# A transformer block on one core: GpSimd's elementwise work on VectorE, a norm's squares in two slots, the fold of a maximum in its own slot, weights fetched one step ahead

## The chip, the core and the metric

The kernel runs on one core of a Trainium2 chip. Its engines have the names of the profile: PE multiplies matrices, DVE (VectorE) and ACT (ScalarE) work element by element, POOL is GpSimd, SP only issues transfers. The metric is the device time of one execution in microseconds; the time before is a median of three runs.

## The reference

The input `x` is float32, 4 sequences of 1024 rows of 512 (D). A vector of 128 numbers for each sequence gives scale `g` and shift `b` of two norms.

```python
def norm(x, t, gw, gb, bw, bb):
    g = (t @ gw.T + gb)[:, None, :]
    b = (t @ bw.T + bb)[:, None, :]
    return g * x * rsqrt(mean(x * x, axis=-1) + 1e-6) + b

def attention(x):                       # 16 heads of 32
    q, k, v = heads(x @ Wq.T), heads(x @ Wk.T), heads(x @ Wv.T)
    p = softmax(q @ k.T / sqrt(32))
    return merge(p @ v) @ Wo.T

def swiglu(x):                          # hidden size 2048
    return silu(x @ gate_w.T) * (x @ hid_w.T) @ out_w.T

x2 = x + attention(norm(x, t, g1w, g1b, b1w, b1b))
out = x + x2 + swiglu(norm(x2, t, g2w, g2b, b2w, b2b))
```

## The kernel before

All tensors lie with features on the 128 partitions, in C = 4 chunks, and with rows on the free axis. The 4096 rows form 8 blocks (`n`) of 512, two for each sequence (`b`, `half`).

**The main loop.** One step `g` handles the scores of four heads, 256 queries and two tiles of 128 keys: `scores(g)` on PE into the one scores bank of PSUM, `keep(g)` on ACT, which copies them to a tile `raw` (nine buffers), and `running_max(g)` on DVE. Four steps (`kind = g % 4`) make a unit `j`: four heads, 256 queries, all 1024 keys. A block has 32 steps and the loop 256, with ten more to drain it. What follows for a unit is spread over later steps:

- `fold_max(j)` halves the running maximum on DVE, `max_T` transposes it on PE (tile `mt`, in the scores bank), `parts` and `parts_T` split it into three bfloat16 parts and transpose them back, `spread` broadcasts the result to `shift`. All of it stands in the kind-0 and kind-1 steps of the next unit.
- Five steps after its scores, `shifted(r)` subtracts the maximum on DVE and `exponential(r)` follows on ACT. One step later `weighted(r)` multiplies by the values on PE and `accumulate(r)` adds the tile into the first `raw` tile of the unit by an accumulating DMA issued from POOL.
- `fold_sum`, `sums` (PE), and `normalize(j)` (a reciprocal on DVE and a multiply on POOL, which writes `oT`) finish the unit.

**What fills PE.** Between these pieces the loop places chains of matmuls into PSUM, 16 short ones each (`mm` splits a matmul into four of 32 columns). They come from two lists: `queue` (projections of keys, queries and values, then the feed-forward `hidden` and `contract` of finished blocks) and `first` (four output projections `project_out` of a block, due eight steps after the block's end). A credit gives two chains per step at the start and 1.6 later. One chain stands in the middle of a step and is evicted there; the other, `late`, stands at its end and is evicted at the start of the next step. Each chain's result occupies one of three PSUM buffers until its eviction: on ACT in the projections (`st`, `sv`), on DVE or on ACT and DVE in the feed-forward part (`h`, `res`).

**The norms.** `norm_squares` makes four squares on ACT and adds them on POOL, `norm_root` averages them with a matmul (`pm`) and takes the root on ACT, `norm_inverse` and `norm_scale` multiply by its reciprocal on DVE, `norm_mod` applies `g` and `b` on ACT. For the attention norm of later sequences (`y`) they hang at steps before `s`, for the feed-forward norm (`x2`) at steps `g0+10` to `g0+16`, where `g0` is the step at which the block's attention steps have ended. `after` hangs a piece at a step's end, `between` in its middle, `pin` at its start.

**Order and queues.** PE, DVE, ACT and POOL execute their instructions in the order in which the program records them. SP's queue (all weight and activation loads and stores) is ordered by the tile framework. Weights of `wkq`, `wo` and `fw` share three buffers. A weight load is recorded with the chain that uses it first.

Of the kernel before, what the change touches and what calls it, by code (L numbers as in the profile page):

```python
# [17 lines left out]
P = 128  # L18
# [6 lines left out]
def tile_cond_transformer_block(  # L25
# [82 lines left out]
    def norm_squares(dst, tag: str):  # L108
        total = None
        for c in range(C):  # L110
            sq = sb.tile([P, NB], F32, tag="t", name=f"sq{tag}_{c}", bufs=3)
            nc.scalar.activation(sq, dst[:, c, :], AF.Square)
            if c == 0:
                total = sb.tile([P, NB], F32, tag="tot", name=f"tot{tag}", bufs=1)
                first = sq
            elif c == 1:
                nc.gpsimd.tensor_tensor(total, first, sq, ALU.add)
            else:
                nc.gpsimd.tensor_tensor(total, total, sq, ALU.add)  # L119
        state[tag] = total  # L120
# [11 lines left out]
    def norm_scale(dst, tag: str):  # L132
        inv = state.pop(tag)
        for c in range(C):
            nc.vector.tensor_tensor(dst[:, c, :], dst[:, c, :], inv, ALU.mult)
# [22 lines left out]
    def norm_rest(which: int, b: int, dst, tag: str):  # L158
        inv = state.pop(tag)
        for c in range(C):  # L160
            nc.vector.tensor_tensor(dst[:, c, :], dst[:, c, :], inv, ALU.mult)
            norm_mod(which, b, dst, c)
# [180 lines left out]

    def normalize(j: int):

        m, qh = divmod(j, NB // HQ)
        n, hg = divmod(m, C)
        rec = sb.tile([P, HQ], F32, tag="rec", name=f"rec{j}", bufs=2)
        nc.vector.reciprocal(rec, state.pop(("sum", j)))  # L349
        if qh == 0:  # L350
            oT[n, hg] = sb.tile([P, NB], F32, tag=f"oT{hg}", name=f"oT{m}")
        nc.gpsimd.tensor_tensor(oT[n, hg][:, qh * HQ : (qh + 1) * HQ], avs.pop(j), rec, ALU.mult)  # L352
# [5 lines left out]
    def project_out(n: int, d: int):  # L358
# [10 lines left out]
        def evict():  # L369
            nc.vector.tensor_tensor(x2[n][:, d, :], pp, res[n][:, d, :], ALU.add)  # L370
            nc.gpsimd.tensor_tensor(res[n][:, d, :], res[n][:, d, :], x2[n][:, d, :], ALU.add)
# [11 lines left out]
    def hidden(n: int, f: int, a: int):  # L383

        if a == 0:
            load_f(n, f)
# [49 lines left out]
    def chains_of(b: int, half: int):  # L436
        todo = []
        for hg in range(C):
            todo.append((load_wkq, project_kq, (b, hg, 0, half)))
# [10 lines left out]
    for hg in range(1, C):  # L450
        enqueue(0, load_wkq, project_kq, (0, hg, 0, 0))
        enqueue(0, None, project_kq, (0, hg, 0, 1))
        enqueue(0, None, project_kq, (0, hg, 1, 0))
    for hg in range(C):
        enqueue(0, load_wkq, project_kq, (0, hg, 1, 1))
    for b in range(1, B):
        for half in range(QB):
# [4 lines left out]
            pin(s - 9, load_y, b, half)  # L462
            after(s - 7, lambda b=b, half=half, tag=tag: norm_squares(y[b, half], tag))
            between(s - 5, norm_root, tag)
            after(s - 4, norm_inverse, tag)
            after(s - 3, lambda b=b, half=half, tag=tag: norm_scale(y[b, half], tag))
            for c in range(C):
                after(s - 2 + c // 2, lambda b=b, half=half, c=c: norm_mod(0, b, y[b, half], c))
            for load, fn, a in chains_of(b, half):
                enqueue(s, load, fn, a)  # L470
    for n in range(NBLK):
# [4 lines left out]
        if n < NBLK - 1:  # L476
            tag = f"f{n}"
            after(g0 + 10, lambda n=n, tag=tag: norm_squares(x2[n], tag))
            between(g0 + 12, norm_root, tag)
            after(g0 + 13, norm_inverse, tag)  # L480
            after(g0 + 14, lambda n=n, tag=tag: norm_scale(x2[n], tag))
# [5 lines left out]
        for g in range(NF // FG):  # L487
            for k in range(FG):
                for a in range(2):
                    enqueue(g1, None, hidden, (n, g * FG + k, a))  # L490
# [4 lines left out]
    for m in range(NBLK * C):  # L495
        pin(m * MS + 4, load_v, m)

    def chain(g: int):
# [5 lines left out]
        if load is not None:  # L504
            load(a[1])
        return fn(*a)

    with tc.manual_schedule(
# [8 lines left out]
        load_modw(1)  # L517
        norm_sum(y[0, 0], "a0_0")
# [27 lines left out]
        while g < NR + 10 or pinned or ended:  # L546
# [13 lines left out]
            if kind == 0 and n_on:  # L560
                normalize(j_n)
            if kind == 3 and s_on:
                fold_sum(j_s)
            if x_on and kind != 1:
                shifted(r_x)
            if late is not None:
                late()
                late = None
            for fn, a in pinned.pop(g, []):
# [14 lines left out]
            if kind == 0 and m_on:  # L584
                fold_max(j_m)
# [10 lines left out]
            if evict is not None:  # L596
                evict()
            for fn, a in halfway.pop(g, []):
# [78 lines left out]
```

## Time and profile before

| | before |
|---|---|
| median of three runs | 2567.27 us (2566.82 to 2568.72) |
| profiled execution, its own time | 2566.51 us |
| span of its profile | 2564.7 us |
| busy: PE, DVE, ACT, POOL | 2470.7, 1764.4, 1309.0, 457.0 us |
| mean granted clock of PE | 0.991 |
| accumulating transfers on POOL's queue | 192 of 1024 KB, 8.3 us from issue to landing |
| weight loads `fw`, `wkq`, `wo` on SP's queue | 3.7, 5.0, 5.6 us from issue to landing (medians) |

In the groups, a line gives the kernel's line, engine, operation, the tiles written and read, partitions and elements, the count, then busy time and mean ns of one, then the idle time before them and what ended it. In the waits, a line gives the waiting engine, tile and line, whom it waited for, and total us, times, and the longest. The timeline gives start and duration in us, and in brackets the idle time before the instruction. A window's line gives its length, the busy time of PE, weight loads, DVE, ACT and POOL with counts, then PE's granted clock, the DMA engines' busy share and GB/s. PE's counts are twice the program's, since one float32 matmul is recorded as two.

### The profile page before, as it was taken

What the parts mean: (1) busy time and instruction counts of PE and PEld (TensorE: products, weight loads), DVE (VectorE), ACT (ScalarE), POOL (GpSimd) and SP (SyncE); (2) the same over time, 40 slices, a digit from 0 to 9 for tenths busy, and PEclk for the clock granted to TensorE, in tenths of its full rate; (3) what the DMA queues carried; (4) which work ended last, traced back from release to release, by engine and by line L of the source; (5) the groups of instructions that cost most, each with busy time, mean ns of one, the idle gap of its engine ahead of it and who ended that gap; (6) DMA issues with size and microseconds to landing.
All of it is one profiled execution on the core that took longest, in us unless ns stands there. A gap on an engine that the chain in (4) does not pass through costs nothing.

```text
span 2564.7 us, 51339 instructions
## 1 busy us (share of the span) xinstructions
PE 2470.7 (96%) x22976; PEld 1005.3 (39%) x22976; DVE 1764.4 (69%) x1465; ACT 1309.0 (51%) x1165; POOL 457.0 (18%) x335
## 2 busy tenths in 40 slices
PE   8999999989999999999989999999999999999999
PEld 3333333334433443344434443344334433333444
DVE  2465666677878788878777878877878778762221
ACT  3566766555555555655555556555555555541000
POOL 0012221211131113111221112111311131111000
PEclk9999999989999999999999999999999999999999
DMA  5678777767767776777668776776687767763221
GB/s 193 184 190 211 195 194 194 175 161 169 168 150 200 174 169 159 187 177 170 160 155 197 166 161 166 195 174 162 150 199 173 162 150 185 175 155 91 89 81 48
DMA packets 125931, 424.08 MB, mean 165 GB/s; under 512 B 12176, under 2 KB 36752, under 8 KB 99216
## 3 DMA queue, kind: packets, MB, share of 16 engines
q0 software_dynamic: 27648, 201.34, 40.5%
q1 hardware_dynamic: 97776, 219.45, 26.0%
q8 instruction: 181, 2.97, 0.4%
q14 instruction: 38, 0.31, 0.0%
q10 hardware_dynamic: 288, 0.01, 0.0%
HBM read 185.87 MB, written 33.55 MB: 86 GB/s over the span
## 4 chain that ended last, share of the span: by engine, by line
PE 81%; DVE 7%; issue 5%; DMA 3%; ACT 2%; POOL 2%; ACTq 0%; SPq 0%; POOLq 0%; DVEq 0%
PE ph L101 29%; PE pc L101 14%; PE sc L235 9%; PE pkq L101 8%; PE av L309 8%; PE pv L101 4%; PE po L101 4%; DVE raw L294 3%; PE mt L262 3%; DMA raw<-raw 2%; DVE rmax L256 1%; PE sp L289 1%; POOL totf L119 1%; DVE rec L349 1%; ACT raw L299 1%
## 5 line engine op out<-in xcount | busy, mean ns | idle before, releaser
L101 PE MATMUL ph<-x,fw 128*32 128x512 f32 (+1 forms) x6488 | 916.5, 593 | 3.4 <-ACT x L138 2.2
L294 DVE TENSOR_TENSOR raw<-raw,shift 128x2048 f32<-128x2048 f32 x256 | 589.4, 2302 | 130.8 <-ACT shift L290 130.8
L242 ACT COPY raw<-sc 128x2048 f32<-128x2048 f32 x256 | 479.5, 1873 | 334.8 <-PE sc L235 189.7
L299 ACT ACTIVATE raw<-raw 128x2048 f32<-128x2048 f32 x256 | 490.3, 1915 | 183.6 <-DVE raw L294 183.4
L101 PEld LDWEIGHTS ph<-x,fw 128*32 128x32 f32 (+1 forms) x6488 | 298.5, 117 | 504.5 <-issue 471.8
L101 PE MATMUL pc<-h,ow 128*32 128x512 f32 (+1 forms) x3184 | 459.4, 593 | 8.1 <-DVE h L398 8.1
L252 DVE TENSOR_TENSOR rmax<-rmax,raw 128x2048 f32<-128x2048 f32 x128 | 298.3, 2330 | 122.0 <-ACT raw L242 121.8
L323 POOL DMA_DIRECT2D raw<-raw x192 | 165.8, 863 | 1056.5 <-ACT raw L299 529.8
L235 PE MATMUL sc<-kq 32*128 32x256 f32 x4096 | 295.6, 403 | 2.8 <-ACT raw L242 2.8
L309 PE MATMUL av<-raw,v 128*32 128x256 f32 x4096 | 276.6, 388 | 15.9 <-ACT raw L299 11.2
L352 POOL TENSOR_TENSOR oT<-avs,rec 128x256 f32<-128x256 f32 x64 | 167.5, 2617 | 570.4 <-DVE rec L349 570.4
L235 PEld LDWEIGHTS sc<-kq 32*128 32x128 f32 x4096 | 186.0, 185 | 168.2 <-issue 133.6
L101 PE MATMUL pkq<-y,wkq 128*32 128x512 f32 (+1 forms) x1808 | 236.7, 608 | 15.7 <-ACT sv L205 5.9
L101 PEld LDWEIGHTS pc<-h,ow 128*32 128x32 f32 (+1 forms) x3184 | 149.7, 118 | 257.7 <-issue 229.0
L396 DVE SCALAR_TENSOR_TENSOR h<-t,ph 128x512 f32<-128x512 f32 x128 | 87.9, 687 | 186.3 <-ACT t L394 186.2
L394 ACT ACTIVATE t<-ph 128x512 f32<-128x512 f32 x128 | 75.7, 592 | 225.8 <-PE ph L101 225.8
L309 PEld LDWEIGHTS av<-raw,v 128*32 128x32 f32 x4096 | 107.8, 109 | 142.2 <-issue 47.2
L250 DVE TENSOR_TENSOR rmax<-raw,raw 128x2048 f32<-128x2048 f32 x64 | 146.3, 2285 | 24.4 <-ACT raw L242 24.4
L410 DVE SCALAR_TENSOR_TENSOR res<-pc,res 128x512 f32<-128x512 f32 x128 | 87.9, 686 | 103.5 <-PE pc L101 103.4
L280 ACT COPY mT<-pt 12x256 bf16<-12x256 bf16 x64 | 23.2, 362 | 259.4 <-PE pt L278 259.4
L398 DVE TENSOR_TENSOR h<-ph,h 128x512 f32<-128x512 f32 x128 | 87.8, 686 | 80.5 <-PE ph L101 80.3
L101 PEld LDWEIGHTS pkq<-y,wkq 128*32 128x32 f32 (+1 forms) x1808 | 71.6, 116 | 151.6 <-issue 132.1
(80 smaller groups left out, 1554.6 us busy)
## 6 DMA issues: line engine op xcount, KB each, us to landing
raw<-raw POOLq DMA_DIRECT2D x192, 1024.0 KB, 8.3
fw<-in_gh_w SPq DMA_DIRECT2D x128, 512.0 KB, 3.7
ow<-in_out_w SPq DMA_DIRECT2D x128, 256.0 KB, 4.2
wkq<-in_kq_w SPq DMA_DIRECT2D x32, 512.0 KB, 5.0
v<-vs SPq DMA_DIRECT2D x32, 512.0 KB, 6.9
kq<-kqs SPq DMA_DIRECT2D x31, 512.0 KB, 7.6
kqs<-st SPq DMA_DIRECT2D x61, 256.0 KB, 5.0
res<-in_x SPq DMA_DIRECT2D x8, 1024.0 KB, 8.2
```

Source lines behind the costliest of these rows:

```text
L101: nc.tensor.matmul(dst[k : k + n, :], w[:, k : k + n], moving, start=start, stop=stop)
L235: nc.tensor.matmul(sc[:, i, k, :], t[rows, kt * P : (kt + 1) * P], t[rows, q0 : q0 + HQ], start=True, stop=True)
L242: nc.scalar.copy(raw[r], state.pop(("sc", r)))
L250: nc.vector.tensor_tensor(rmax[j], raw[r - 1], raw[r], ALU.max)
L252: nc.vector.tensor_tensor(rmax[j], rmax[j], raw[r], ALU.max)
L294: nc.vector.tensor_tensor(t, t, shift[r // UN].unsqueeze(2).to_broadcast([P, HG, 2, HQ]), ALU.add)
L299: nc.scalar.activation(raw[r], raw[r], AF.Exp)
L309: nc.tensor.matmul(av[j][i * DH : (i + 1) * DH, :], v[m][:, kt, i * DH : (i + 1) * DH], raw[r][:, i, k, :], start=(kt == 0), stop=(kt == K ...
L323: nc.gpsimd.dma_start(out=acc[j].rearrange("p h k q -> p (h k q)"), in_=raw[r].rearrange("p h k q -> p (h k q)"), accum_op=ALU.add,)
L352: nc.gpsimd.tensor_tensor(oT[n, hg][:, qh * HQ : (qh + 1) * HQ], avs.pop(j), rec, ALU.mult)
L396: nc.vector.scalar_tensor_tensor(h[n, f], t, 1.0, pp, ALU.add, ALU.mult)
L410: nc.vector.scalar_tensor_tensor(r, pp, 0.5, r, ALU.mult, ALU.add)
```

## The change

- `norm_squares` is called for two chunks at a time, in two consecutive steps, and its adds are on DVE. Load, root, inverse, scaling and `norm_mod` of the attention norm move one or two steps earlier; root of the feed-forward norm one step; its scaling is split over two steps.
- The multiply of `normalize` and the residual add in `project_out` go from POOL to DVE. POOL keeps the accumulating transfers.
- In the kind-0 step the eviction of `late` now comes first, then the reciprocal (`inverse`), `shifted`, and the multiply; before it was reciprocal, multiply, `shifted`, and the eviction.
- `fold_max` moves from the kind-0 step to the end of the kind-3 step before it.
- `fetch` records a weight load with the chain before the one that used to record it: one load stays ahead.

```diff
-    def norm_squares(dst, tag: str):
-        total = None
-        for c in range(C):
-            sq = sb.tile([P, NB], F32, tag="t", name=f"sq{tag}_{c}", bufs=3)
-            nc.scalar.activation(sq, dst[:, c, :], AF.Square)
...
-                nc.gpsimd.tensor_tensor(total, first, sq, ALU.add)
-            else:
-                nc.gpsimd.tensor_tensor(total, total, sq, ALU.add)
-        state[tag] = total
+    def norm_squares(dst, tag: str, k: int):
+
+        sq = [sb.tile([P, NB], F32, tag="t", name=f"sq{tag}_{2 * k + i}", bufs=3) for i in range(2)]
+        for i in range(2):
+            nc.scalar.activation(sq[i], dst[:, 2 * k + i, :], AF.Square)
+        if k == 0:
+            state[tag] = sb.tile([P, NB], F32, tag="tot", name=f"tot{tag}", bufs=1)
+            nc.vector.tensor_tensor(state[tag], sq[0], sq[1], ALU.add)
+        else:
+            for t in sq:
+                nc.vector.tensor_tensor(state[tag], state[tag], t, ALU.add)
...
+    def inverse(j: int):
+        rec = sb.tile([P, HQ], F32, tag="rec", name=f"rec{j}", bufs=2)
+        nc.vector.reciprocal(rec, state.pop(("sum", j)))
+        state["rec", j] = rec
...
-        nc.gpsimd.tensor_tensor(oT[n, hg][:, qh * HQ : (qh + 1) * HQ], avs.pop(j), rec, ALU.mult)
+        nc.vector.tensor_tensor(oT[n, hg][:, qh * HQ : (qh + 1) * HQ], avs.pop(j), rec, ALU.mult)
...
-            nc.gpsimd.tensor_tensor(res[n][:, d, :], res[n][:, d, :], x2[n][:, d, :], ALU.add)
+            nc.vector.tensor_tensor(res[n][:, d, :], res[n][:, d, :], x2[n][:, d, :], ALU.add)
...
-            pin(s - 9, load_y, b, half)
-            after(s - 7, lambda b=b, half=half, tag=tag: norm_squares(y[b, half], tag))
-            between(s - 5, norm_root, tag)
-            after(s - 4, norm_inverse, tag)
-            after(s - 3, lambda b=b, half=half, tag=tag: norm_scale(y[b, half], tag))
+            pin(max(s - 10, 0), load_y, b, half)
+            for k in range(2):
+                after(s - 8 + k, lambda b=b, half=half, tag=tag, k=k: norm_squares(y[b, half], tag, k))
+            between(s - 6, norm_root, tag)
+            after(s - 5, norm_inverse, tag)
             for c in range(C):
-                after(s - 2 + c // 2, lambda b=b, half=half, c=c: norm_mod(0, b, y[b, half], c))
+                between(s - 4, lambda b=b, half=half, tag=tag, c=c: norm_scale(y[b, half], tag, c))
+                after(s - 4 + c // 2, lambda b=b, half=half, c=c: norm_mod(0, b, y[b, half], c))
...
-            after(g0 + 10, lambda n=n, tag=tag: norm_squares(x2[n], tag))
-            between(g0 + 12, norm_root, tag)
+            for k in range(2):
+                after(g0 + 9 + k, lambda n=n, tag=tag, k=k: norm_squares(x2[n], tag, k))
+            between(g0 + 11, norm_root, tag)
             after(g0 + 13, norm_inverse, tag)
-            after(g0 + 14, lambda n=n, tag=tag: norm_scale(x2[n], tag))
+            for c in range(C):
+                after(g0 + 14 + c // 2, lambda n=n, tag=tag, c=c: norm_scale(x2[n], tag, c))
...
+    def fetch():
+
+        if loads:
+            load, a = loads.popleft()
+            load(*a)
...
         if load is not None:
-            load(a[1])
+            fetch()
...
-            if kind == 0 and n_on:
-                normalize(j_n)
             if kind == 3 and s_on:
                 fold_sum(j_s)
-            if x_on and kind != 1:
+            if x_on and kind in (2, 3):
                 shifted(r_x)
             if late is not None:
                 late()
                 late = None
+            if kind == 0:
+                if n_on:
+                    inverse(j_n)
+                if x_on:
+                    shifted(r_x)
+                if n_on:
+                    normalize(j_n)
...
-            if kind == 0 and m_on:
-                fold_max(j_m)
...
             if evict is not None:
                 evict()
+            if kind == 3 and g < NR:
+                fold_max(g // UN)
```

## The prediction

> **What bounds the kernel now.** I read the page first (busy shares, clock row), then PE's waits, the groups with their shapes kept apart, the windows of 64 us, and the timeline around the block boundaries.
>
> ```profile
> PE 2470.7 (96%) x22976; PEld 1005.3 (39%) x22976; DVE 1764.4 (69%) x1465; ACT 1309.0 (51%) x1165; POOL 457.0 (18%) x335
> PEclk9999999989999999999999999999999999999999
> ```
>
> PE is busy 96%. Its work does not change, so the most that any edit can win is PE's idle time, 2564.7 - 2470.7 = 94 us, and the time in which its clock was down. PE's own waits say who causes the idle time:
>
> ```profile
> PE mt L262 <- DVE rmax L256: 18.2, 18, 5.0
> PE mt L262 <- ACT raw L242: 13.0, 6, 5.8
> PE av L309 <- ACT raw L299: 11.2, 9, 3.0
> PE pc L101 <- DVE h L398: 8.1, 4, 2.9
> PE pkq L101 <- ACT sv L205: 5.9, 2, 3.0
> PE pkq L101 <- DMA wkq<-in_kq_w: 5.7, 1, 5.7
> ```
>
> Eighteen waits for the folded maximum, mostly 0.4 to 1.1 us; the others are few and long. The timeline puts the long ones in the step groups after each block's output projection. The worst, at block 3:
>
> ```profile
> 1282.50 6.50 POOL L119 TENSOR_TENSOR totf<-totf,sqf 128x512 f32<-128x512 f32 x2
> 1288.94 0.87 POOL L323 DMA_DIRECT2D raw<-raw  x1
> 1295.95 1.87 ACT L242 COPY raw<-sc 128x2048 f32<-128x2048 f32 x1 [9.30 <-DMA raw<-raw]
> 1297.87 1.97 PE L262 MATMUL mt<-ident,rmax 128*128 128x128 f32 x8 [5.80 <-ACT raw L242]
> ```
>
> POOL runs its queue in order. The accumulating transfer of `raw` stands behind the adds of the norm's squares, so it leaves at 1288.94; the copy of the next scores needs the buffer that it frees, waits 9.30 us, and PE stands 5.80 us for the copy. The windows show what such a gap costs besides, in their column of the granted clock (the last but two):
>
> ```profile
> 256.00:320.00 64.00, 62.35 (x626) 23.43 (x630) 42.33 (x27) 44.96 (x47) 13.62 (x12) 0.97 0.76 194
> 512.00:576.00 64.00, 55.61 (x559) 23.28 (x553) 44.20 (x38) 35.78 (x32) 9.49 (x7) 0.89 0.66 163
> 1280.00:1344.00 64.00, 54.73 (x524) 22.91 (x520) 48.20 (x42) 33.31 (x31) 18.61 (x11) 0.95 0.61 147
> ```
>
> A mean clock of 0.95 over 64 us is 3.2 us of PE work lost; 0.89 is 7.0, 0.97 is 1.9.
>
> **The change part by part.** What moves from POOL to DVE, and the rows that price it:
>
> ```profile
> L352 POOL TENSOR_TENSOR oT<-avs,rec 128x256 f32<-128x256 f32 x64 | 167.5, 2617 | 570.4 <-DVE rec L349 570.4
> L371 POOL TENSOR_TENSOR res<-res,x 128x512 f32<-128x512 f32 x32 | 54.1, 1699 | 87.8 <-DVE x L370 87.8
> L119 POOL TENSOR_TENSOR totf<-totf,sqf 128x512 f32<-128x512 f32 x14 | 37.9, 2708 | 1.1
> L135 DVE TENSOR_TENSOR x<-x,invf 128x512 f32<-128x512 f32 x28 | 17.4, 684 | 0.0
> L331 DVE TENSOR_TENSOR raw<-raw 128x1024 f32<-128x1024 f32 x64 | 80.9, 1264 | 3.2 <-DMA raw<-raw 3.2
> L256 DVE TENSOR_TENSOR rmax<-rmax 128x1024 f32<-128x1024 f32 x64 | 93.8, 1466 | 0.0
> ```
>
> *DVE's new load.* The 39 adds of squares (14+7 for the feed-forward norms, 12+6 for the attention norms) and the 32 residual adds have L135's form: 71 x 684 ns = 48.6 us. For the 64 multiplies 128x256 no DVE row has the size; from L135 to L331 an element costs (1264-684)/512 = 1.13 ns, so 684 - 256x1.13 = 0.39 us; upper bound 0.68 us, L135's own. I take 0.39: 25 us. Sum 74 us, DVE 1764 to 1838 us, 72%. L256 has L331's size but lies beside POOL's multiply and takes 0.2 us more; if that goes, 64 x 0.2 = 13 us come back. In a steady group of four steps DVE's rows add up to some 27 us against 33.5 us of PE (a block of 32 steps takes 268 us in the timeline), so there it lies beside PE. At the boundaries the cover is thin, see 4.
>
> *1. Fold in its own slot.* Fold now follows the last running maximum, a step before the transposes. Of the 18.2 us of waits I leave 5.0 (block 0) and 2.5 (block 5, where DVE is late anyway) out: **gain 10.5 us**. The step that takes the fold also has the fold of sums: 1.26+2.3+2.33+1.26 and evictions of 0.69 each, about 8.2 us against 8.4; it just fits.
>
> *2. POOL's queue is left with the 192 transfers alone.* The accumulation no longer waits for 8 us of adds; its data was ready at 1278.1, when the exponential before it ended, 10.8 us before it left; with 7 us to land, the buffer is free at about 1286, before the scores of that step are done. Gone are the waits of `mt` for the scores copy at blocks 2 to 5: 2.67+5.80+1.56+1.41 = 11.4 us, and the 3.2 us of clock: **gain 14.6 us**.
>
> *3. Squares in two slots of two.* In the projection stage four squares on ACT, one held up by POOL, stood before the eviction `sv`; PE waited twice 2.96 us for it, and each window lost 1.9 us of clock. Now at most two squares (1.24 us) stand there, and the scaling of `y` has moved to other steps: **gain 9.7 us**. Inverse root one step earlier: its table load leaves the step of the `shift` copies; counted in 4.
>
> *4. DVE lateness after each output projection.* Waits for `h`, for an exponential behind a late DVE and for late folds: at 780, 1055, 1331, 1591, 1605, 1867, 1874, 2136 and 2143 us, together 18.6 us, and 3.8 us of clock. The change takes from it (scaling in two halves; table load and fold moved) and adds to it: per block four residual adds, three square adds and two multiplies, 2.7+2.1+0.8 = 5.6 us in eight steps. My sum for DVE there is 64.5 us against 67 of PE, before 59; and each slot of squares makes DVE wait for ACT (1.2 us). Bounds: all 22 us gone, or 5.6 us more on each of seven blocks, -39 us. DVE is busy 77% of the time in these stretches (347 of 452 us over seven of them), so there is slack still: I take a third of the waits, **gain 7 us**, and a **loss of 3 us** for new short waits (`pt` behind the parts).
>
> *5. Block 0.* 512 to 530 us: 8.4 us of waits and 7.0 us of clock. PE has no projection left there and waits for DVE's chain of reciprocal, shift, fold; only the fold leaves it: **gain 2 us**.
>
> *6. Reciprocal and multiply after the late eviction, multiply after the shift.* The output projection needs the last `oT` some 4.7 us after its step's scores begin (1.1 + 1.0 + three quarters of 3.4). POOL's multiply began at 985.08, before the scores at 985.74. Now an eviction (0.69), reciprocal (1.75), shift (2.23) and 0.39 come first: 5.1 us, and 6.4 where the eviction waits for a tanh (at 987.06 in the trace). Waits of 0.4 to 1.7 us, eight blocks: **loss 7 us**.
>
> *7. Weights a step ahead.* SP's queue is not ordered by hand; in the built program it differs little: one early weight load, and per block a feed-forward load ahead of an output weight, which then waits for the buffer just used. That one still has some 12 us before its first use, against 5.6 us to land (9.4 at most). The one weight wait, 5.7 us at 119 us, comes behind the load of `y`, which waits on SP for its buffer; that order is the same: **0 us** (bounds -3 and +8).
>
> Sum: 10.5+14.6+9.7+7+2-3-7 = 34 us less.
>
> [...] After the 5.80 us gap the window is at 0.95, but windows with only 2.96 us gaps lose 1.9 us too. [...] if DVE were saturated, 74 us would come onto the path, and the sum be +74-44 = 30 us slower. DVE is at 69%, and at 77% in the boundary stretches: not saturated. I keep the lower sum[...].
>
> **The rivals.**
> A (0.60), as summed: 2515 to 2550 us.
> B (0.14), the gaps were all POOL's doing: part 4 is won whole, parts 6 and the new waits cost nothing: 10.5+14.6+9.7+22.4+2 = 59, about 2508, down to 2490 if clock losses elsewhere go too. For it: gaps follow the held transfer. Against: 2.98 us at 1591 comes behind a 3.35 us reciprocal on DVE.
> C (0.12), half the gain: PE, no longer stopped in part 2, meets DVE's lateness earlier, so that parts 2 and 4 are given back: 34 - 14.6 - 7 = 12 us, about 2555. For it: the late DVE waits of block 3 and 4 follow right on the gaps that go. Against: DVE's wait for ACT's table load, which starts that lateness at 1583, goes as well.
> D (0.14), DVE becomes the bound at the boundaries and in the fold's step. Parts 1 to 3 and 5 win 37 us; they are used up once each of seven blocks costs 5.3 us more than before, just what 5.6 us of added DVE work would cost with no slack. With part 6 and the fold's step (0.2 us each over 64 groups, 13 us): 39+7+13-37 = 22 us slower, 2589. Lighter forms end between 2560 and 2575. For it: 64.5 of 67 us is thin. Against: the next 16 steps of each block, where DVE has 6 us of slack in every four steps and catches up.
>
> **The numbers.** The profiled execution took 2566.51 us (span 2564.7 and 1.8 around it), the median is 0.8 above: 2567.3 - 34 = 2533. 0.2% is 5 us, about what the three runs (2566.82 to 2568.72) can tell. Faster by more than that: A, B and C, 0.86. D's 0.14 is split: its lighter forms within 0.2% 0.05, slower 0.09. The range holds A, C and half of B, and leaves out the rest of B (0.07) and D: 2505 to 2560.
>
> **What would show it.** Right: no wait of `mt` for `rmax`; no copy of scores waiting 9 us for `raw`; the `sv` waits gone; PE busy near 2462, with the clock at 1.00 after block 3 and the dip of block 0 (the 8 in the clock row) still there; new waits of `po` for `oT` on DVE, 1 us each; the 5.7 us `wkq` wait still there. Wrong: PE waiting for `h` or `raw` by over 5 us per block (D), or no waits there at all (B).

## The result, and the profile after

The changed kernel takes 2549.45 us (median of six runs, 2545.06 to 2551.1) against 2569.97 us for the kernel before on the same chip (2566.82 to 2574.8): ratio 0.9916, 95% interval 0.9902 to 0.9931, some 21 us faster. The forecast was 34. The profiled execution took 2551.1 us (span 2549.3, granted clock 0.990).

The sum of the forecast was made against the profiled execution of before, and the two profiled spans differ by 2564.7 - 2549.3 = 15.4 us. Times of one kernel spread over 6 to 8 us here; the profiled execution of after is the slowest of its six, and that of before (2566.51 us) is quicker than any of the six timed ones. So what is compared step by step below adds up to 15.4 us, and the medians give 21.

The page after, its busy times and its clock row:

```profile
PE 2473.6 (97%) x22976; PEld 1003.2 (39%) x22976; DVE 1803.1 (71%) x1600; ACT 1311.6 (51%) x1165; POOL 166.4 (7%) x200
PEclk9999999999999999999999999999999999999999
```

PE is 3 us busier with the same instructions. It stands idle 71.4 us in its waits, 88.8 before. Its clock is no better: the time at half clock in the trace's clock records costs 27.0 us, 24.6 before. So between these two executions all of the gain is idle time. (The clock differs from one execution to the next: the six of the changed kernel have 0.989 to 0.992.) PE's waits after (us in total, times, longest):

```profile
PE pt L273 <- DVE split L268: 13.7, 9, 4.0
PE av L304 <- ACT raw L294: 6.9, 7, 3.0
PE po L101 <- DMA wo<-in_vo_w: 6.0, 1, 6.0
PE pkq L101 <- DMA wkq<-in_kq_w: 5.5, 1, 5.5
...
PE pc L101 <- DVE h L395: 5.4, 4, 2.3
PE mt L257 <- ACT raw L237: 5.1, 4, 2.1
...
PE po L101 <- DVE oT L351: 4.2, 7, 1.0
```

The two waits that led the list of before, `mt` for the fold and for the copy of scores (18.2 and 13.0 us), are down to 0 and 5.1. The wait for `sv` (5.9 us) is gone. Three rows are worse or new: `pt` for the parts was 4.8 us and is 13.7; `po` waits once for a weight load, 6.0 us; and `po` waits for `oT`, 4.2 us in seven waits, as forecast.

At block 3, where PE stood 5.80 us before, the timeline (start, duration) now shows the transfers and the copy of scores on time:

```profile
1270.21 0.86 POOL L318 DMA_DIRECT2D raw<-raw  x1 [14.35 <-ACT raw L294]
...
1279.87 0.86 POOL L318 DMA_DIRECT2D raw<-raw  x1 [8.80 <-issue]
1280.51 1.86 ACT L237 COPY raw<-sc 128x2048 f32<-128x2048 f32 x1
1283.11 1.09 PE L257 MATMUL mt<-ident,rmax 128*128 128x128 f32 x8
```

Neither the copy nor the transpose has a wait in brackets. The same three windows of 64 us as before, and two that got worse (columns: PE, PEld, DVE, ACT, POOL busy, then the granted clock):

```profile
256.00:320.00 64.00, 64.00 (x670) 24.25 (x666) 47.94 (x35) 44.34 (x47) 4.30 (x5) 1.00 0.78 209
512.00:576.00 64.00, 62.15 (x620) 24.31 (x620) 46.09 (x40) 34.60 (x29) 4.30 (x5) 0.93 0.63 143
960.00:1024.00 64.00, 57.06 (x570) 22.72 (x567) 47.07 (x44) 33.53 (x27) 4.31 (x5) 0.95 0.58 130
1280.00:1344.00 64.00, 60.75 (x612) 24.51 (x608) 53.88 (x49) 38.16 (x34) 5.02 (x6) 1.00 0.74 181
1536.00:1600.00 64.00, 59.12 (x573) 23.40 (x568) 50.67 (x48) 35.50 (x32) 4.30 (x5) 0.95 0.72 169
```

Window 256 was 62.35 at 0.97, window 1280 was 54.73 at 0.95: won. Window 960 was 62.84 at 1.00: the new weight wait lies there. Window 1536 was 58.28 at 1.00: the wait behind a late VectorE (2.99 us) is as it was, and now costs clock too.

VectorE's new work is priced by its groups (busy us, mean ns):

```profile
L351 DVE TENSOR_TENSOR oT<-avs,rec 128x256 f32<-128x256 f32 x64 | 26.4, 412 | 0.0
L370 DVE TENSOR_TENSOR res<-res,x 128x512 f32<-128x512 f32 x32 | 22.1, 692 | 1.1
L251 DVE TENSOR_TENSOR rmax<-rmax 128x1024 f32<-128x1024 f32 x64 | 78.0, 1218 | 0.4
```

0.41 and 0.69 us are the durations of the forecast. But VectorE's busy time grew by 39 us, not by 74 or 61: its old instructions became faster, the fold from 1466 to 1218 ns and more besides (last section).

### The profile page after: what moved, and what is told of

It is laid out like the page before. It is cut to its first block, busy times and chain, and to the rows that moved or that the text cites. A ratio compares the mean times of both kernels' runs of the same rounds, so it can differ in the third digit from the quotient of the medians.

```text
span 2549.3 us, 51152 instructions
## 1 busy us (share of the span) xinstructions
PE 2473.6 (97%) x22976; PEld 1003.2 (39%) x22976; DVE 1803.1 (71%) x1600; ACT 1311.6 (51%) x1165; POOL 166.4 (7%) x200
## 5 line engine op out<-in xcount | busy, mean ns | idle before, releaser
L289 DVE TENSOR_TENSOR raw<-raw,shift 128x2048 f32<-128x2048 f32 x256 | 581.3, 2271 | 108.8 <-ACT shift L285 108.8
L247 DVE TENSOR_TENSOR rmax<-rmax,raw 128x2048 f32<-128x2048 f32 x128 | 292.9, 2288 | 89.7 <-ACT raw L237 88.8
L101 PE MATMUL po<-oT,wo 128*32 128x512 f32 (+1 forms) x856 | 117.5, 605 | 10.2 <-DMA wo<-in_vo_w 6.0
```

The lines of the kernel that those rows point to most:

```text
L101: nc.tensor.matmul(dst[k : k + n, :], w[:, k : k + n], moving, start=start, stop=stop)
L247: nc.vector.tensor_tensor(rmax[j], rmax[j], raw[r], ALU.max)
L289: nc.vector.tensor_tensor(t, t, shift[r // UN].unsqueeze(2).to_broadcast([P, HG, 2, HQ]), ALU.add)
```

## The experiments

Each was timed against the kernel before on the same chip. Differences are (ratio - 1) x 2570 us, so that kernels of different chips can be set side by side; for the changed kernel this gives 22 us where the medians gave 21. The intervals are 3 to 4 us to each side (2 in run 8), so two rows can be told apart from some 5 us on.

| kernel | ratio to before, 95% | against before |
|---|---|---|
| changed kernel | 0.9916 [0.9902, 0.9931] | -22 us |
| 1 own loads | 0.9893 [0.9880, 0.9907] | -27 us |
| 2 old order of the kind-0 step | 0.9924 [0.9911, 0.9938] | -20 us |
| 3 fold back in the kind-0 step | 1.0057 [1.0044, 1.0069] | +15 us |
| 4 square adds on GpSimd | 0.9949 [0.9937, 0.9962] | -13 us |
| 5 residual adds on GpSimd | 0.9926 [0.9914, 0.9939] | -19 us |
| 6 own loads, reciprocal in halves | 0.9843 [0.9830, 0.9856] | -40 us |
| 7 own loads, root a step later | 0.9874 [0.9859, 0.9889] | -32 us |
| 8 before, with the fold's move alone | 0.9986 [0.9980, 0.9993] | -4 us |
| 9 before, with the squares alone | 0.9949 [0.9935, 0.9964] | -13 us |
| 10 own loads, halves, root later | 0.9817 [0.9803, 0.9830] | -47 us |
| 11 old order and fold in the kind-0 step | 0.9963 [0.9950, 0.9976] | -10 us |
| 12 multiply of `oT` on GpSimd | 0.9886 [0.9870, 0.9901] | -29 us |

### 1: each weight load with its own chain

```diff
         if load is not None:
-            fetch()
+            load[0](*load[1])
         return fn(*a)
...
         load_modw(1)
-        fetch()
```

> The changed kernel (2549.5 us) with each weight load recorded with its own chain again. Theory: the fetch ahead costs one wait, 6.0 us of PE for the second output weight of block 2, plus 3.4 us of half clock after it; nothing else of it shows. Then 9 us faster than the changed kernel, about 2540, and no wait of po for wo. Rival: the wait covers DVE's lateness after the output projection, which shows as soon as PE no longer stands: 3 to 5 us faster, with new waits for h or raw in block 2. Third: the fetch ahead pays elsewhere, and its removal costs: slower, with waits for fw or wkq.

Measured: 2543.12 us, about 6 us less than the changed kernel. PE's wait for `wo` is gone, and window 960 is back at 63.07 us of PE and a clock of 1.00. Of the other waits one grows (`ph` for `h` at 743 us, 1.0 to 2.7 us) and two shrink, so that waits are 6.3 us less in all. Behind block 0 the clock loses 5.2 us less, as expected or better, but in this execution 3.4 us more in the first 150 us, where the two kernels wait alike (see the last section). So the early fetch is a loss of about 6 us net, and the cause is this place in the timeline of the changed kernel:

```profile
984.01 0.86 POOL L318 DMA_DIRECT2D raw<-raw  x1 [8.71 <-DMA raw<-raw]
985.81 0.56 SPq L363 DMA_DIRECT2D wo<-in_vo_w  x1
...
994.40 9.29 PE L101 MATMUL po<-oT,wo 128*32 128x512 f32 x64 [6.01 <-DMA wo<-in_vo_w]
```

The three buffers of the weights hold `fw` of the chain in progress, `fw` fetched ahead, and the first half of `wo`. The second half must take the buffer of the first, and its load can only be issued when the second output projection has ended (985.8). Its first use was due at 994.40 - 6.01 = 988.4, not 12 us but 2.6 us later. It also leaves 1.8 us behind an accumulating transfer of 1 MB, and takes 8.5 us to land.

### 2, 3 and 11: order and fold, as a square

Edit 2 restores the order of before in the kind-0 step, edit 3 the fold's place, 11 both:

```diff
# 2: order
-            if x_on and kind in (2, 3):
-                shifted(r_x)
+            if kind == 0 and n_on:
+                inverse(j_n)
+                normalize(j_n)
+            if x_on and kind != 1:
+                shifted(r_x)
             if late is not None:
                 late()
                 late = None
-            if kind == 0:
-                if n_on:
-                    inverse(j_n)
-                if x_on:
-                    shifted(r_x)
-                if n_on:
-                    normalize(j_n)
# 3: fold
+            if kind == 0 and m_on:
+                fold_max(j_m)
...
-            if kind == 3 and g < NR:
-                fold_max(g // UN)
```

> The changed kernel with the kind-0 step in its former order: reciprocal, multiply (still on DVE), shift, and the late eviction last. Theory: the order of the change makes the multiply and the parts late, PE waits 4.2 us for oT and 13.7 us for the parts (4.8 before): about 10 us faster than the changed kernel, 2540, with both waits near those of before (0 and 5). Rival: a late eviction frees h and PSUM later, and PE waits for h instead: within 3 us of the changed kernel.

> The changed kernel with the fold of the maximum back in the kind-0 step. Theory: the waits of mt for rmax return, 18 us and more since the multiply stands ahead of it now: 18 to 25 us slower than the changed kernel, 2567 to 2575. Rival: PE waits for the parts in that step anyway (13.7 us), and the fold's own slot makes DVE late in the step before; then only 5 to 10 us slower.

> The changed kernel with the old order of a kind-0 step and the fold back in that step: the fourth corner beside the changed kernel, the old order alone and the fold back alone. If the fold's place is worth little under the old order, as the fold alone on the kernel before says (4 us), it takes 2555 to 2560, ratio 0.994 to 0.996, and the 36 us that the fold costs under the new order are the order's doing, an interaction. Rival: the fold's place is worth 20 us or more once GpSimd's adds are gone, whatever the order; then 2573 or more, ratio over 1.001.

Against before, in us:

| | fold in kind 0 | fold in its own slot |
|---|---|---|
| old order | -10 (run 11) | -20 (run 2) |
| new order | +15 (run 3) | -22 (changed kernel) |

Under the old order the fold's move is worth 10 us, give or take 5, which agrees with the step's 10.5. Run 11 expected about 4 from run 8; that guess was probably too small, and its rival of 20 or more is out. Under the new order the same move is worth 36 us, more than the 18 to 25 expected. PE's waits in run 3 say it in one row:

```profile
PE mt L257 <- DVE rmax L251: 47.8, 51, 6.0
```

51 waits, most of them short, instead of the 18 of before. Run 11, with the old order, has 22 of them (29.9 us). In both orders the fold stands behind the same four pieces: reciprocal, multiply, shift and late eviction. What differs is which of them comes first, and VectorE's trace has them in the order of the program in both. The same step in run 3 and then in run 11:

```profile
823.64 1.15 PE L230 MATMUL sc<-kq 32*128 32x256 f32 x16
824.40 0.69 DVE L393 SCALAR_TENSOR_TENSOR h<-t,ph 128x512 f32<-128x512 f32 x1 [2.55 <-ACT t L391]
829.15 1.22 DVE L251 TENSOR_TENSOR rmax<-rmax 128x1024 f32<-128x1024 f32 x1
830.52 1.06 PE L257 MATMUL mt<-ident,rmax 128*128 128x128 f32 x8 [1.30 <-DVE rmax L251]
```

```profile
814.25 1.75 DVE L341 RECIPROCAL rec<-sum 128x256 f32<-128x256 f32 x1
816.12 1.15 PE L230 MATMUL sc<-kq 32*128 32x256 f32 x16
819.18 1.22 DVE L251 TENSOR_TENSOR rmax<-rmax 128x1024 f32<-128x1024 f32 x1
821.63 1.09 PE L257 MATMUL mt<-ident,rmax 128*128 128x128 f32 x8
```

With the eviction first, VectorE stands idle 2.55 us for ScalarE's tanh of the late chain, and everything behind moves; the fold begins 5.5 us after the scores of its step. With the reciprocal first, VectorE works through that time, and the fold begins 3.1 us after the scores. The order by itself is worth 2 us with the fold out of the way, within the error of the two ratios, and costs 24 us with the fold behind it. In run 2 the wait of `po` for `oT` is gone, as meant, but `pt` for the parts rises from 13.7 to 17.3 us and `pc` for `h` from 5.4 to 8.4. The rival of that run held: the old order pays what it saves. So the two edits belong together: the new order needs the fold gone.

### 8 and 9: the fold alone and the squares alone, on the kernel before

```diff
# 8, on the kernel before
-            if kind == 0 and m_on:
-                fold_max(j_m)
...
+            if kind == 3 and g < NR:
+                fold_max(g // UN)
# 9, on the kernel before: norm_squares and norm_scale of the changed kernel, and its steps
-            after(s - 7, lambda b=b, half=half, tag=tag: norm_squares(y[b, half], tag))
-            between(s - 5, norm_root, tag)
+            for k in range(2):
+                after(s - 8 + k, lambda b=b, half=half, tag=tag, k=k: norm_squares(y[b, half], tag, k))
+            between(s - 6, norm_root, tag)
...
-            after(g0 + 10, lambda n=n, tag=tag: norm_squares(x2[n], tag))
-            between(g0 + 12, norm_root, tag)
+            for k in range(2):
+                after(g0 + 9 + k, lambda n=n, tag=tag, k=k: norm_squares(x2[n], tag, k))
+            between(g0 + 11, norm_root, tag)
```

> The kernel before (2569.9 us) with the fold of the maximum in its own slot as the only edit. Theory: the 18.2 us of waits of mt for rmax go, of which 10 to 12 us are short ones that nothing replaces: 10 to 15 us faster than before, 2556 to 2560. Rival, since putting the fold back cost the changed kernel 36 us: most of the change's gain is the fold, 20 us. Second rival: the parts are then what PE waits for in the same step, and 5 us remain.

> The kernel before with parts 2 and 3 alone: squares and scaling of the norms in two slots, their adds on VectorE, the norm's root and reciprocal at the new steps. The fold, the order of a kind-0 step, the multiply of oT and the residual adds (GpSimd) stay as before. By the prediction's terms 14.6 + 9.7 = 24 us faster than before (about 2546, ratio 0.9905). Rival, from the fold alone having brought 4 us where 10.5 were forecast: a removed wait comes back in part as a later one or as clock, then 8 to 15 us faster. Told apart by PE's waits: sv and the 5.8 us copy of scores must be gone in both; under the rival the waits for h and the exponential grow, or the clock stays near 0.990 with less idle time.

Run 8 gains 4 us where 10 to 15 were expected, run 9 gains 13 where 24 were: in both the theory of separate terms missed, and the rival held. PE's waits of run 9 show where a removed wait comes back:

```profile
PE mt L257 <- DVE rmax L251: 28.8, 20, 6.2
PE av L304 <- ACT raw L294: 7.3, 8, 3.0
PE ph L101 <- DVE h L391: 6.2, 2, 3.6
```

The waits for `sv` and for the copy of scores are gone (the latter has 0.5 us left), but `mt` waits 28.8 us for the fold where it waited 18.2: PE comes to the transposes earlier, and VectorE isn't earlier with the fold. In run 8 the fold's 18.2 us are gone, `pt` behind the same chain rises from 4.8 to 9.9 us, and idle time is 7.4 us less in all; but in the profiled execution the clock loses 36.7 us instead of 24.6. That execution is the second slowest of 21, at a clock of 0.986 where their median is 0.989 (0.991 before), so the usual loss is smaller: some 4 us of the 7 are left as gain. Both runs hold less than their terms: a removed wait uncovers the next one in its chain. All of the change holds 22 us against 17 for the sum of the two, and 27 without the early fetch (run 1). The first difference is within the error; the second is not, but it also holds the new order and the moves of the multiply and the residual adds. So it suggests, and does not prove, that the two terms need each other.

### 4, 5 and 12: one kind of elementwise work back on GpSimd

```diff
# 4
-            nc.vector.tensor_tensor(state[tag], sq[0], sq[1], ALU.add)
+            nc.gpsimd.tensor_tensor(state[tag], sq[0], sq[1], ALU.add)
...
-                nc.vector.tensor_tensor(state[tag], state[tag], t, ALU.add)
+                nc.gpsimd.tensor_tensor(state[tag], state[tag], t, ALU.add)
# 5
-            nc.vector.tensor_tensor(res[n][:, d, :], res[n][:, d, :], x2[n][:, d, :], ALU.add)
+            nc.gpsimd.tensor_tensor(res[n][:, d, :], res[n][:, d, :], x2[n][:, d, :], ALU.add)
# 12
-        nc.vector.tensor_tensor(oT[n, hg][:, qh * HQ : (qh + 1) * HQ], avs.pop(j), rec, ALU.mult)
+        nc.gpsimd.tensor_tensor(oT[n, hg][:, qh * HQ : (qh + 1) * HQ], avs.pop(j), rec, ALU.mult)
```

> The changed kernel with the adds of the squares on POOL, still in two slots of two. Theory: what counts is POOL's queue; the last two adds, some 6 us, hold the accumulating transfer back, and the copy of the scores waits for raw again at the block boundaries: 5 to 14 us slower than the changed kernel. Rival: DVE is the bound at the boundaries, and 2.1 us less of it per block help: 3 to 8 us faster. Third: two slots were all that mattered: no difference.

> The changed kernel with the 32 residual adds back on POOL (22 us less for DVE, 2.8 us per block, all of it in the stretch after the output projection). Theory A: DVE is the bound in that stretch, and the waits for h, for exponentials and for the parts there (some 20 us) shrink: 5 to 10 us faster than the changed kernel. Theory B: those waits come from single places in the order (the 3.35 us reciprocal ahead of a shift, a full set of PSUM buffers), not from DVE's total: within 3 us. Theory C: the adds, up to 4.5 us a pair on POOL, hold an accumulating transfer back again: 3 to 8 us slower.

> The changed kernel with the multiply of oT alone back on GpSimd, in its new place in the order. It tells two things. First, whether VectorE's large instructions were held up by GpSimd's two-input multiply: then the running maximum's 128x1024 form goes back from 1.22 to about 1.45 us and VectorE's busy time falls by much less than the multiply's own 26 us. If not, it stays at 1.22. Second, the price of the wait of po for oT: GpSimd's 2.6 us in place of 0.4 should add about 2.2 us to each of seven or eight waits, 15 to 18 us, and the accumulating transfers stand behind the multiplies again: 10 to 25 us slower than the changed kernel (ratio 0.995 to 1.002). Rival: the multiply is off the path everywhere, within 5 us of the changed kernel.

The squares are 8 us worse on GpSimd, within the 5 to 14 us that the queue explanation gave them. In the trace that explanation is seen in part only: one of the four waits for a copy of scores comes back, at block 3 (1.6 us; 5.8 before), and `mt` for the copy rises from 5.1 to 7.0 us in all, of 4.8 us of added idle time; the rest stands in the rows of `h`, `res` and `pt`. The residual adds make no difference that can be told: taking 22 us of work from VectorE buys nothing, although this run also meets the load of `wo` in a better moment (`po` waits 1.4 us for it); `ph` for `h` rises from 2.9 to 6.2 us. And the multiply, the largest of the three, is better on GpSimd, by some 8 us. Run 12 expected a loss of 10 to 25 us or, by its rival, a difference within 5; both missed. Its 2.6 us cost PE hardly more than VectorE's 0.41 did: `po` waits 6.1 us for `oT` instead of 4.2. And the timeline shows what made the difference:

```profile
983.58 0.56 SPq L363 DMA_DIRECT2D wo<-in_vo_w  x1
...
985.41 0.85 POOL L318 DMA_DIRECT2D raw<-raw  x1 [6.64 <-DMA raw<-raw]
...
987.39 7.07 PE L101 MATMUL po<-oT,wo 128*32 128x512 f32 x64 [1.23 <-DMA wo<-in_vo_w]
```

Compare with the same three lines of the changed kernel under run 1. There the 1 MB transfer was issued 1.8 us ahead of the load of `wo`, here 1.8 us behind it. The load takes 3.7 us to land instead of 8.5, and PE waits 1.2 us instead of 6.0, at full clock. Run 5 has a load of 3.8 us with no transfer issued in the 11 us ahead of it; run 11 has one of 9.1 us, with a transfer 0.2 us ahead. So 5 of these 8 us are the weight wait, met by chance in a better moment, and the 3.4 us of half clock behind it make up the rest; they aren't an argument for GpSimd. Run 1 agrees: with the multiply on VectorE and no weight wait it stands at 0.9893, beside 0.9886 here.

### 6, 7 and 10: the norm of the feed-forward part

What is left after each output projection was traced to VectorE's reciprocal of 128x512 and to the step in which the root stands. The edits, on top of run 1:

```diff
# 6
+    def norm_half(tag: str, i: int):
+        t = state[tag][:, i * HQ : (i + 1) * HQ]
+        nc.vector.reciprocal(t, t)
...
-            after(g0 + 13, norm_inverse, tag)
+            for i in range(2):
+                after(g0 + 12 + i, norm_half, tag, i)
# 7
-            between(g0 + 11, norm_root, tag)
+            between(g0 + 12, norm_root, tag)
```

> Own loads (2543 us) and the reciprocal of the feed-forward norm in two halves of 256 columns, at the ends of two steps instead of one of 3.35 us. Theory: the long reciprocal stands ahead of the next step's shift; the wait of 2.98 us in block 4 and the waits for h two steps on (2.3 and 1.7 us in blocks 1 and 2) get smaller by 1.6 us each, and one stretch of half clock goes: 5 us faster than own loads, 2538. Rival: DVE's total is the bound there, and halves change nothing (within 2 us).

> Own loads (2543 us) and the mean and root of the feed-forward norm one step later, as before the change. Theory: in the step of the sums the three PSUM buffers are held by a chain, the sums and the mean, so the next chain waits for DVE to empty one (h or res: 2.7, 1.9, 1.6 us in blocks 1, 4, 5); later, these waits go: 4 to 6 us faster than own loads, 2538. Rival: the table load of the root is back in the step of the shift copies, and the exponential two steps on is late by 1.3 us: up to 5 us slower.

> The changed kernel with own loads, the feed-forward norm's reciprocal in two halves, and its root one step later, all three together. If the two last gains (about 13 and 7 us against own loads alone) are separate, 2521 or so, ratio about 0.981. Rival: the root one step later puts the two half reciprocals right behind it in the same step, so that the scaling is late; then no better than the halves alone, 0.984 to 0.987.

Halves: 13 us less than run 1, more than double the 5 expected. (The halves stand at the ends of two steps, so one of them also comes a step earlier than the whole did; the split and the earlier place were not timed apart.) Root later: 5 us less, as expected. Both: 20 us less than run 1, so the two are separate, and run 10 at 2525.41 us (2524.26 to 2525.86) is the fastest kernel here, 1.8% under before and 1% under the changed kernel. VectorE around block 4, in the changed kernel and in run 10:

```profile
1565.82 3.34 DVE L128 RECIPROCAL invf<-invf 128x512 f32<-128x512 f32 x1
1569.09 2.23 DVE L289 TENSOR_TENSOR raw<-raw,shift 128x2048 f32<-128x2048 f32 x1
```

```profile
1551.28 1.74 DVE L132 RECIPROCAL invf<-invf 128x256 f32<-128x256 f32 x1
1552.94 2.23 DVE L293 TENSOR_TENSOR raw<-raw,shift 128x2048 f32<-128x2048 f32 x1
```

The shift begins 1.6 us sooner behind the half. PE's wait for the exponential behind it falls from 2.99 to 1.39 us. In PE's waits `h` and `res` together fall from 13.3 us in run 1 (4.6, 4.7, 2.4, 1.6) to 9.6 with the halves alone, to 7.0 with the later root alone, and to 2.2 in run 10:

```profile
PE av L308 <- ACT raw L298: 5.0, 6, 1.4
...
PE ph L101 <- DVE h L397: 1.2, 2, 0.6
PE pc L101 <- DVE h L399: 1.0, 2, 0.7
```

The halves take the rows of `pc` for `h`; the later root takes those of `res` and most of `ph` for `h`. The gain is larger than the waits because gaps of over 2 us became gaps of about 1, and in these traces no slow cell follows a cell with under 1.5 us of idle time (see the last section): the clock loses 19.7 us in run 10, 25.2 in run 1. (For run 6 alone the trace shows 16.2, but 5.1 of its 9 us fall in the first 150 us, where the two kernels wait alike; see the last section.)

## Why the prediction was right, and where its sum was off

The sign and the waits named in steps 1 to 3 held. The size did not: 34 us were summed, 15.4 us are there between the two profiles and 21 between the medians. The median of 2549 us lies in the range of case A by less than 1 us, and nearer to the 2555 of case C than to A's sum of 2533; that A's range holds it is in part luck. By its own steps, idle time and clock from the two traces:

| step | forecast, us | measured, us |
|---|---|---|
| 1 fold in its own slot | +10.5 | +10.7 |
| 2 POOL's queue | +14.6 | +14.6 |
| 3 squares in two slots | +9.7 | +9.7 |
| 4 lateness after output projections | +7 - 3 | -8 |
| 5 block 0 | +2 | +1 |
| 6 new order, `po` for `oT` | -7 | -4 |
| 7 weights a step ahead | 0 | -9 |
| sum | 34 | 15 |

**Steps 1 to 3** were read from waits that the change plainly takes away, and these waits went: no `rmax`, no `sv`, none of the four copies of scores at blocks 2 to 5, and the clock of windows 256, 320 and 1280 at 1.00. But run 8 and run 9 show that the terms are not worth this one at a time (4 and 13 us), so the table's first lines are true of the whole change only.

**Step 4 is the term that failed most**, by 12 us. It took "a third of the waits" as won. The list that was summed to 18.6 us before (waits for `h`, `res`, an exponential behind a late VectorE, a late fold or parts, each of 0.9 us or more) comes to 21.5 us after, and the clock in the windows of 704, 1536, 2048 and 2112 us loses 8.9 us, where two windows lost 3.8 (both from the rounded clock of the windows, as in the forecast). VectorE was not too busy there: run 5 takes 22 us of work away to no effect, and runs 6, 7 and 10 remove the waits without taking any. What holds PE is single instructions that stand in front of others at the wrong moment, the 3.34 us reciprocal above all; the change left it where it was. And one of the step's reasons had the wrong sign: the root a step earlier was counted as a help (each table load takes ScalarE 1.28 us in the traces of before and after), yet run 7, which puts it back, is 5 us faster than run 1 (and run 10 is 7 us faster than run 6), and PE's 4.0 us of waits for `res` are gone there. The 3 us for new short waits named the right row, `pt` behind the parts, and undersized it: it rose by 8.9 us, 1.8 of them in block 0, 4.7 in two long waits of the list above and 2.4 in short ones elsewhere. With the fold early, PE meets the same chain one link later.

**Step 7** was set at 0, with a loss of 8 at most; it cost 9.2, 6.0 of wait and 3.2 of clock in window 960. Run 1 gets 6 of them back. The step that failed is "some 12 us before its first use". It was read from the distance in steps, and not from the buffer: with one load held ahead, the last of three buffers comes free 2.6 us before the use. Two things then work against it that the working named apart and did not join: the load cannot leave earlier, and step 2 had just made the 1 MB transfer leave on time, in front of it.

**Step 6** has the right wait in the right place, 4.2 us in seven waits of up to 1.0 us, where eight of 0.4 to 1.7 had been summed.

**Step 5** held in kind: its waits go from 8.4 to 7.3 us, where 2 were to be won, and the four slow cells of the clock (6.8 us) are as before. So is the 5.5 us wait for `wkq`.

**The tests of the forecast** are met by the waits; "PE busy near 2462" is not (2473.6), because the clock loss moved and did not shrink (27.0 us, 24.6 before), and the 8 in the clock row is gone though the dip in block 0 is there (0.93 in its window). **Rival D**, VectorE as the bound, is out: 71% busy, 39 us more work and no wait of 5 us per block. **Rival B** needed all lateness to be POOL's doing; it is VectorE's order. **Rival C** had the mechanism of step 4's failure in it: PE is stopped less in part 2 and meets VectorE's lateness earlier. It gave back step 4 and more, as C had it, but not step 2, whose waits stay won.

## What to carry to other kernels

A wait that goes is worth its length only if the engine that released it, or the next one in its chain, is early enough for what comes after (in run 8 waits of 18.2 us went and 4 us were gained): sum the terms, then ask of each which wait stands one link behind it. A load fetched ahead occupies a buffer, so count from the moment that the buffer comes free to the first use, and look at which large transfer leaves just before (the load of `wo` took 8.5 us to land behind one, 3.7 when issued ahead of one). Where the waiting engine's releaser is only 70% busy, look for the one long instruction in front of the needed one and cut it in two before moving work to another engine (run 6 gained 13 us, with one half a step earlier; run 5 moved 22 us of work and gained nothing). And where one engine's order is changed, ask which instruction put first waits for another engine: in run 3 all that stands behind the eviction waited with it, 2.55 us in the step shown.

## What the runs showed of the hardware

**Of two gaps of the same length, one cost clock.** The forecast read from its windows that gaps of nearly 3 us cost clock. Two traces have the same gap at the same place; one pays and the other does not. First the kernel before: PE's wait, and two stretches of 3.41 us around it.

```profile
1026.97 1.09 PE L262 MATMUL mt<-ident,rmax 128*128 128x128 f32 x8 [2.67 <-ACT raw L242]
```

```profile
1022.53:1025.95 3.42, 1.77 (x20) 0.26 (x9) 3.42 (x2) 0.90 (x1) 3.09 (x2) 1.00 0.99 236
1025.95:1029.36 3.41, 2.39 (x12) 1.68 (x13) 2.17 (x4) 3.39 (x3) 0.41 (x1) 1.00 0.85 186
```

Then run 8:

```profile
1026.07 1.97 PE L262 MATMUL mt<-ident,rmax 128*128 128x128 f32 x8 [2.66 <-ACT raw L242]
```

```profile
1022.01:1025.42 3.41, 1.39 (x16) 0.19 (x8) 3.41 (x3) 1.27 (x1) 2.60 (x2) 1.00 0.84 211
1025.42:1028.83 3.41, 2.76 (x10) 2.25 (x11) 0.80 (x2) 3.39 (x3) 0.85 (x2) 0.50 0.74 159
```

In the clock records of before and after the clock is at 1.00 or at 0.50. Before, nine stretches at 0.50 lie in the span: six of 3.41 us, two of 6.83 and one of 13.65, and their starts, from 15.60 to 2135.28 us, lie whole multiples of 3.41 us apart. A stretch of this grid of 3.41 us is called a cell here, and a slow cell when it is at 0.50. In the kernel before, the gap of 2.67 us lies across a border of the grid, 1.65 and 1.02 us to the sides, and the clock stays at 1.00. In run 8 the gap of 2.66 us lies with 2.02 us in one cell (PE busy 1.39 of 3.41), and the next cell runs at 0.50: the eight transposes take 1.97 instead of 1.09 us. Counted from 150 us on, in cells that were not slow themselves:

| PE idle in the cell | slow cell behind it: before and after | all fourteen traces |
|---|---|---|
| under 1.5 us | 0 of 1365 | 0 of 9538 |
| 1.5 to 2 us | 3 of 10 | 14 of 66 |
| 2 to 2.5 us | 4 of 5 | 41 of 43 |
| above 2.5 us | 5 of 5 | 30 of 30 |

A slow cell costs up to half of its 3.41 us, 1.7 us of PE work. These are counts of this case's traces; what sets the clock was not shown.

So in these traces the clock terms of the forecast go with a wait and its phase on the grid, not with a wait alone, and any earlier change shifts all later gaps. The grid is not tied to the start of the kernel either: its first slow cell begins at 15.60 us of the span before and at 15.89 after. In the first 150 us, where all fourteen kernels wait nearly alike, half clock costs 5.1 us in five traces, 6.8 in two (before and after) and 10.2 in seven. A difference of up to 5 us of clock between two traces therefore needs no edit to explain it, and the spread of one kernel's times is of that size (6.0 us after, 8.0 before). That is how the profiled execution of run 8 could lose 12 us more of clock while 7 us of idle time were gone. A version with few gaps over 2 us, like run 10 (two after block 0), has little left to lose that way; its clock loses 19.7 us in all. Waits of 2.0 to 3.1 us cost clock in part of the cases: of 86 single ones after the first 150 us that did not begin at half clock, 53 had a slow cell right behind one that they touched. In before and after it is 8 of 15, and both waits of 2.96 us on which the forecast's step 3 rests are among the eight.

**Beside some of GpSimd's instructions, VectorE's took longer.** In the kernel before, a shift of 128x2048 beside the adds of squares took

```profile
1281.19 3.38 DVE L294 TENSOR_TENSOR raw<-raw,shift 128x2048 f32<-128x2048 f32 x1
```

against 2.28 us alone, the mean of 176; of the running maxima of that size, six beside GpSimd's adds averaged 3.18 us and 122 others 2.29. The evictions of 128x512, which read PSUM, did not take longer: 38 beside the adds or the multiply averaged 0.68 us, the 346 others 0.69. With the adds and the multiply on VectorE, 75 us of added work (71 x 0.69 and 64 x 0.41) made it only 39 us busier: the fold, the shifts, the running maxima and the folds of sums together take 32 us less. It took most of the force from rival D. The shift that began ahead kept its time: in run 12 the multiply of 128x256 is issued 0.2 us behind the start of the shift, takes 2.6 us itself, and the shift keeps its 2.23 us. In the kernel before, 63 shifts begin 0.17 us ahead of the multiply and average 2.23 us, and seven begin 0.17 us ahead of a residual add and keep 2.28, while that add takes 3.24 us instead of 1.27. The fold, which has its own slot in run 12, averages 1220 ns there. In the kernel before, the 30 folds that overlap the multiply by 0.65 to 0.67 us average 1750 ns, the 34 others, with under 0.1 us of overlap, 1216, and all of them 1466. Its place alone is not the cause: in run 3, with the fold back in the kind-0 step and the multiply on VectorE, it averages 1219.

**What the records count.** In the kernel before, the scores' float32 matmuls, eight in each of 256 steps, have 4096 records, two each; the transposes `mt`, eight in each of 64 units, have 512, one each.
